# Moving turns, router, adapter and stores at the second and third meeting of sequences

## Chip, core and metric

One NeuronCore of a Trainium2 chip runs the whole kernel in one launch. The metric is the device time of the launch in microseconds (us), lower is better. The kernel is written by hand down to the order in which instructions are issued; each engine works off its own queue in that order, and semaphores let engines wait for each other.

## The reference

The input `x` is four sequences of 1024 rows and 1024 columns in float32. What is computed, cut to the main steps:

```python
x = x + attn(layernorm(x), wq, wk, wv, wo)     # 32 heads of 32, rotary q and k, causal softmax
x = x + ffn(layernorm(x), route_w, A, Bw)

def ffn(x, route_w, A, Bw):                     # 8 experts, rank 16, the best one only
    logits = einsum('bsd,ed->bse', x, route_w)
    topk_v, topk_idx = top_k(logits, 1)
    route_weight = one_hot(topk_idx[..., 0], 8) * topk_v
    h = einsum('bsd,erd->bser', x, A)
    return einsum('bser,eor->bso', route_weight[..., None] * h, Bw)
```

## The kernel before

Each sequence has eight row tiles of 128 rows and eight groups of four heads. A *unit* is one group of one sequence, so there are 32 units. The kernel works on three things at once. In unit u the scores, the exponentials and the products with the values of group u (and the second half of group u - 1) are made. Into them are woven the q, k and v projections of group u + 1. And, from the second sequence on, one row tile per unit of the sequence before is finished: output product with `wo`, residual, second layernorm, turn, router, adapter, store.

The score work of a unit is a fixed list of eleven slots, `SLOTS`: nine score rounds, with the marks "second" and "first" between them, at which half of a group's values are multiplied (`apply`). Everything else is a list of `Step`s, each with a cost in units of about one product; `fill` takes steps from the list `todo` after each slot until that slot's share of the cost is spent. So a step's place in the list decides beside which score round it is issued. A step can also put work on `postponed`: a pair of a cost and a function, and the function is called once steps of that much cost have gone by.

A *meeting* is the last unit of a sequence (group 7), where the next sequence begins. There are three, in units 7, 15 and 23. The second and third have a list written out by hand in `change_steps`, because six kinds of step meet there:

- `norm.find(t)`, `norm.scale(t)`, `norm.turn(t)` for the row tiles of the next sequence: statistics on DVE (with a power on POOL), scaling on DVE (L189), and eight transposes on PE (L201, `pt_a`), copied out of PSUM by ACT (L203, L205). Every turn of a tile loads another one. Tiles 3, 4 and 6 live for a while in the buffers of the coming qT and kT, so the profile shows them as `qT` and `kT`.
- `h`, the held steps: products of the value projection of unit 15 or 23 (`pv`, L337).
- `p`, the project steps: sixteen output products of the last row tile of the old sequence (`po`, L751), eight for each half of the columns. Each uses a weight chunk, loaded from DRAM into one of four buffers; a product asks for the chunk four places on.
- `turn`, `route`, `turn_hidden` and `adapt` of the row tile before that (tile 6). `turn` is `pt_f`; `route` is a product with the router's and the experts' weights (`ph`, L773) and five small steps on DVE that give `wh`; `turn_hidden` transposes `wh` (`pw`, L802); `adapt` makes two products (`pf`, L812), adds them to `y` on DVE (L815) and stores `y` to `out_y` (L816). On SP the store waits for L815.
- the projections of the next unit (`chains`: `pq`, `pk`, `pv`).
- the score rounds and value products (`s`, L430; `av`, L634), which the slots put between them.

All projection, turn, router and adapter results pass through four PSUM banks (pool `ps`), which are given out again as they come free. Scores and value products have a bank area of their own with one buffer.

DVE also finds the maxima of each score round (L462, L483), transposes the probabilities in place (L516) and the values (L1096), and scales the value products (L654). All DMA is issued by one queue, SP, in program order. Values go out to DRAM and come back rearranged (`spread_values`): four stores `vd<-vT` and eight loads `vals<-vd` per unit. In the main loop `stores` holds the stores of a unit's values and value products, and `scatter` puts the eight loads into `todo`, two steps apart.

Of the kernel before, what the change touches and what calls it, by code (L numbers as in the profile page):

```python
# [14 lines left out]
P = 128  # L15
# [56 lines left out]
def tile_preln_attn_then_top1_lora(  # L72
# [17 lines left out]
    nc = tc.nc  # L90
    B, S, D = x.shape
# [5 lines left out]
    NG = HEADS // HG  # L97
# [17 lines left out]
    def bank(shape, name):  # L115
        return ps.tile(shape, F32, tag="ps", name=name)
# [58 lines left out]
    def find_moments(src, name):  # L175
        stats = small.tile([P, D // 512, nc.vector.BN_STATS_DIM], F32, tag="stats", name=f"st_{name}")
        for i in range(D // 512):
            nc.vector.bn_stats(stats[:, i, :], src[:, i * 512 : (i + 1) * 512])
        mv = small.tile([P, nc.vector.BN_AGGR_DIM], F32, tag="mv", name=f"mv_{name}", bufs=3)
        nc.vector.bn_aggr(mv, stats)  # L180
        ve = small.tile([P, 1], F32, tag="ve", name=f"ve_{name}")
        nc.vector.tensor_scalar(ve, mv[:, 1:2], EPS, None, ALU.add)
        rstd = small.tile([P, 1], F32, tag="rstd", name=f"rstd_{name}", bufs=3)
        nc.gpsimd.tensor_tensor(rstd, ve, half_sb, ALU.pow)
        return mv, rstd
# [41 lines left out]
    postponed = []  # L227
# [19 lines left out]
    class Norm:  # L247
# [32 lines left out]
        def find(self, t):  # L280
            while self.found <= t and self.found in self.x:
                k = self.found
                self.moments[k] = find_moments(self.x[k], f"a{self.b}_{k}")
                self.found += 1
# [26 lines left out]
        def scaling(self, t):  # L311
            return Step(lambda: self.scale(t), 0.0)

        def turning(self, t):
            return Step(lambda: self.turn(t), 2.0 if self.b == 0 else 1.3)
# [169 lines left out]
    def release_exps():  # L485
        to_exp.extend(next_exp)
        next_exp.clear()
# [200 lines left out]
    def load_adapter():  # L688

        ra_all = NC * (E + ER)  # L690
        room = big.tile([P, ra_all + D + TB * D], F32, tag="prob0", name="adapter")
        kept["ra"] = room[:, :ra_all].rearrange("p (c n) -> p c n", n=E + ER)
        kept["bw"] = room[:ER, ra_all : ra_all + D]
        for k in range(TB):
            kept[k] = room[:, ra_all + D + k * D : ra_all + D + (k + 1) * D]
        nc.sync.dma_start(kept["ra"], ra.rearrange("(c p) n -> p c n", p=P))
        nc.sync.dma_start(kept["bw"], bw)
# [13 lines left out]
    def take_chunk(n):  # L711
        for k in range(n, n + 4):
            if k < n + 3 or n == 0:
                load_chunk(k)
        return loaded[n]

    def finish_steps(b, t, kind="stream"):
# [88 lines left out]
        def adapt(ks=None):  # L806
            y = st["y"]
            for n in range(2):
                cols = slice(n * 512, (n + 1) * 512)
                pf = bank([P, 512], f"pf_{name}_{n}")  # L810
                rhs = kept["bw"][:, cols] if ks is None else take_chunk(ks[n])
                nc.tensor.matmul(pf, lhsT=st["whT"], rhs=rhs, start=True, stop=True)  # L812
                if ks is not None:
                    load_chunk(ks[n] + 4)
                nc.vector.tensor_tensor(y[:, cols], pf, y[:, cols], ALU.add)  # L815
            nc.sync.dma_start(out[b, t * P : (t + 1) * P, :], y)  # L816

        def number(step, sources):

# [2 lines left out]
        chains = []  # L822
# [27 lines left out]
    def change_steps(u, norm, project, tail, held):  # L850

        p, h, turning, scaling = project, held, norm.turning, norm.scaling
        out, chains = [], []
        for n, tb in (("q", 0), ("k", 0), ("q", 1), ("k", 1), ("v", 0), ("v", 1)):
            chains += chain(u, n, tb)
        if p:
            turn, route, turn_hidden, adapt = tail
            find = norm.finding  # L860
            load_last = Step(lambda: norm.load(7), 0.0)
            out += [*h[:2], turn, *h[2:4], find(3), p[0], h[4], turning(2), h[5], p[1], route, scaling(3)]
            out += [find(4), h[6], p[2], h[7], p[3], turn_hidden, scaling(4), *p[4:6], adapt, load_last]
            out += [p[6], find(5), p[7], turning(3), scaling(5), *p[8:10], turning(4), *p[10:12]]
            chains = weave(chains[:-6], p[12:]) + chains[-6:]
            out += [*chains[:2], find(6), *chains[2:4], scaling(6), turning(5), *chains[4:6], find(7)]
            out += [*chains[6:8], scaling(7), turning(6), *chains[8:14], turning(7)]
            return out + chains[14:]
        for t, n in zip(range(TB, NT), (3, 4, 4, 4)):
            out += [*chains[:n], turning(t)]  # L870
            del chains[:n]
        return out + chains
# [194 lines left out]
    def scatter(steps, apart):  # L1067

        for k, s in enumerate(steps):
            todo.insert(min(len(todo), 1 + apart * k), s)  # L1070

    n_slots = len(SLOTS)
    second, first_ = SLOTS.index("second"), SLOTS.index("first")
    final = len(units) - 1
    for u, (b, g) in enumerate(units):
        do_postponed(math.inf)
        do_postponed(math.inf)
        todo.extend(between[u])
        ends_at = n_slots
        if b + 1 < B and g + 1 == NG:  # L1080
            if b:
                norms[b + 1].load(3, 4)
        if u == final:
            load_wo()
            ends_at = second
        for r, pieces in enumerate(SLOTS):
            if pieces == "second":
                release_exps()
            if pieces == "second":
                if u == final:  # L1090
                    todo.extend(early)
                    ends_at = second + 3
                put, loads = spread_values(u)

                def meanwhile():
                    nc.vector.transpose(vTs[u], vTs[u])  # L1096
                    if u in ahead_of:
                        ahead_of[u][0]()

                if u:  # L1100
                    apply(u - 1, 1, meanwhile)
                else:
                    meanwhile()
                stores.append(put)
            elif pieces == "first":
                apply(u, 0)
                find_tops(u)
                ended.clear()
            else:
                release_exps()  # L1110
                turn_probabilities()
                if second < r < first_:
                    join_sums(u, 0)
                if r == second + 1 and u in ahead_of:
                    ahead_of[u][1]()
                score_round(u, pieces)
                if r == second - 1 and u:
                    while any((u - 1, t) in places for t in range(QT, 2 * QT)):
                        exponentiate_some(1)
                        turn_probabilities()  # L1120
                    join_sums(u - 1, 1)
                if r != first_ - 1:
                    find_tops(u)
                exponentiate_some(SHARE / 3)
                next_exp.extend((u, t, h) for t in ended for h in range(HG))
                if r != first_ - 1:
                    ended.clear()
                if r in (second + 1, first_ + 1):
                    for put in stores:
                        put()  # L1130
                    stores.clear()
                    if u == final and r == first_ + 1:
                        load_adapter()
                if r == second + 2:
                    scatter(loads, 2)
                    if u in late_fetch:
                        do(late_fetch[u])
                        for k in range(3 if b == 1 else 0):
                            load_chunk(k)
            if u == final:  # L1140
                if r == second + 3:
                    todo.extend(parts)
                    ends_at = first_ + 2
                if r == first_ + 1:
                    todo.extend(wholes)
                    ends_at = n_slots + 2
            held_back = APART_BY if r < second else 0
            ahead = LENGTHS if not b and u + 1 < NG else [1.0] * ends_at
            fill(
                ahead[r] / sum(ahead[r:ends_at]),  # L1150
                held_back,
                0.0 if pieces in ("first", "second") else SHARE * 2 / 3,
            )
# [61 lines left out]
```

## Time and profile before

| | |
|---|---|
| median of 3 runs | 2722.84 us (2721.9 to 2724.6) |
| profiled execution | 2722.25 us |
| its span in the trace | 2720.5 us |
| granted TensorE clock, mean | 0.997 |
| PE busy | 2666.9 us, 98% of the span |
| DVE busy | 2143.7 us, 79% |
| ACT busy | 1723.5 us, 63% |
| POOL busy | 601.4 us, 22% |
| weight chunks `chunk<-in_wo` | 368 issues of 256 KB, 3.8 us to landing (median) |
| stores `out_y<-x` | 32 issues of 512 KB, 2.6 us to landing |

The profile's times are of one execution. Engines are PE (TensorE), DVE (VectorE), ACT (ScalarE), POOL (GpSimd) and SP (the queue that issues DMAs). In a timeline row the first number is the start in us from the start of the span, the second the time that the row's instructions took together, then engine, line, operation, what is written and read, shape and count; a bracket gives the idle time of the engine just before and what ended it. A float32 product of 512 columns appears as two MATMUL records. The windows view gives, for each stretch of time, how long each engine was busy in it, and the granted clock of TensorE as a share of full speed.

### The profile page before, as it was taken

Reading aid. Unit: us, or ns where it says so; the run is one execution under the profiler, and the core shown is the slowest. Engines: PE = TensorE matmul, PEld = TensorE weight load, DVE = VectorE, ACT = ScalarE, POOL = GpSimd, SP = SyncE. Lnnn points to the kernel's source line nnn. Section 1 sums busy time; section 2 is a strip of 40 time slices with the busy share of each in tenths; the row PEclk is TensorE's granted clock in tenths of the full one; section 3 lists DMA queues with packets and bytes.
Section 4 is the critical chain, followed back from the end, with each engine's and each line's share of the span. In section 5 each row is a group of like instructions: output and inputs, shape, how many; then the busy total and the mean of one; then the engine's idle time right before and its main releaser. Section 6 shows DMA issues by size and latency. Waiting matters only on the chain.

```text
span 2720.5 us, 84063 instructions
## 1 busy us (share of the span) xinstructions
PE 2666.9 (98%) x35108; PEld 1302.4 (48%) x35108; DVE 2143.7 (79%) x4256; ACT 1723.5 (63%) x4978; POOL 601.4 (22%) x845
## 2 busy tenths in 40 slices
PE   8999999999999999989999999999999999999998
PEld 5444444444444544445444454444544444544445
DVE  4899989887777788887777877888787777787555
ACT  2878777876666676665666666766566666666521
POOL 2222222222222222222122222222212222212000
PEclk9999999999999999999999999999999999999999
DMA  3222223226554445652555454564355555446421
GB/s 119 60 72 73 75 74 81 64 64 172 149 135 134 126 127 155 168 158 65 161 160 134 135 131 133 137 188 135 80 158 149 154 134 138 120 131 199 126 69 53
DMA packets 465900, 332.74 MB, mean 122 GB/s; under 512 B 160880, under 2 KB 382320, under 8 KB 465520
## 3 DMA queue, kind: packets, MB, share of 16 engines
q1 hardware_dynamic: 465520, 327.37, 44.1%
q8 instruction: 276, 4.52, 0.7%
q14 instruction: 104, 0.85, 0.1%
HBM read 277.01 MB, written 50.26 MB: 120 GB/s over the span
## 4 chain that ended last, share of the span: by engine, by line
PE 79%; DVE 13%; DMA 3%; ACT 3%; POOL 1%; issue 1%; SPq 1%; POOLq 0%; DVEq 0%; ACTq 0%
PE po L751 15%; PE pq L337 14%; PE pk L337 13%; PE pv L337 11%; PE s L430 11%; PE av L634 8%; DVE top L462 4%; DVE pr L516 3%; PE ph L773 2%; PE pf L812 2%; DMA chunk<-in_wo 2%; DVE both L483 1%; ACT pr L441 1%; ACT pr L491 1%; PE pt_f L201 1%
## 5 line engine op out<-in xcount | busy, mean ns | idle before, releaser
L491 ACT ACTIVATE pr<-pr,both 128x256 f32<-128x256 f32 (+15 forms) x2048 | 1044.4, 518 | 51.2 <-DVE both L483 51.2
L441 ACT COPY pr<-s 128x640 f32<-128x640 f32 (+14 forms) x544 | 525.1, 1017 | 670.4 <-PE s L430 669.7
L462 DVE TENSOR_REDUCE top<-pr 128x2 f32<-128x960 f32 (+15 forms) x768 | 650.6, 893 | 253.6 <-POOL pr L444 253.0
L516 DVE STREAM_TRANSPOSE pr<-pr 128x1024 f32<-128x1024 f32 (+11 forms) x768 | 664.8, 907 | 34.5 <-ACT pr L491 31.0
L444 POOL TENSOR_TENSOR pr<-pr,causal_sb 128x128 f32<-128x128 f32 x512 | 237.3, 470 | 1166.8 <-ACT pr L441 1158.2
L337 PE MATMUL pv<-xnT,wv 128*128 128x512 f32 x1024 | 486.3, 602 | 0.0
L337 PE MATMUL pq<-xnT,wq 128*128 128x512 f32 x1008 | 478.2, 602 | 0.2 <-ACT xnT L203 0.2
L337 PE MATMUL pk<-xnT,wk 128*128 128x512 f32 x1008 | 477.9, 603 | 0.0
L430 PE MATMUL s<-kT,qT 32*32 32x256 f32 (+4 forms) x17408 | 394.5, 385 | 8.9 <-POOL pr L444 3.0
L491 ACT ACTIVATION_READ_ACCUMULATOR pr<-pr,both 128x1 f32 x2048 | 401.3, 196 | 0.0
L751 PE MATMUL po<-chunk,attn 128*128 128x512 f32 x736 | 379.2, 600 | 7.5 <-DMA chunk<-in_wo 7.5
L430 PEld LDWEIGHTS s<-kT,qT 32*32 32x32 f32 x17408 | 187.6, 103 | 267.4 <-issue 102.7
L337 PEld LDWEIGHTS pk<-xnT,wk 128*128 128x128 f32 x1008 | 181.4, 190 | 234.9 <-issue 234.5
L337 PEld LDWEIGHTS pq<-xnT,wq 128*128 128x128 f32 x1008 | 183.3, 191 | 225.1 <-issue 223.8
L337 PEld LDWEIGHTS pv<-xnT,wv 128*128 128x128 f32 x1024 | 185.6, 190 | 218.1 <-issue 216.6
L634 PE MATMUL av<-pr,vals 64*32 64x256 f32 (+3 forms) x12288 | 272.0, 319 | 4.6 <-DVE pr L516 3.8
L634 PEld LDWEIGHTS av<-pr,vals 64*32 64x32 f32 x12288 | 214.1, 106 | 112.3 <-issue 66.4
L483 DVE TENSOR_TENSOR both<-top 32x4 f32<-32x4 f32 (+3 forms) x1152 | 207.8, 180 | 23.8
L751 PEld LDWEIGHTS po<-chunk,attn 128*128 128x128 f32 x736 | 134.8, 190 | 173.7 <-issue 147.7
L654 DVE TENSOR_TENSOR at<-av,by 128x256 f32<-128x256 f32 x128 | 48.2, 418 | 108.7 <-PE av L634 70.4
L751 PE MATMUL po<-wo,attn 128*128 128x512 f32 x256 | 116.6, 596 | 0.0
L375 POOL TENSOR_TENSOR qT<-qT,swapq 128x512 f32<-128x512 f32 x64 | 81.6, 1274 | 140.0 <-DVE swapq L371 140.0
(89 smaller groups left out, 1561.9 us busy)
## 6 DMA issues: line engine op xcount, KB each, us to landing
chunk<-in_wo SPq DMA_DIRECT2D x368, 256.0 KB, 3.8
vals<-vd SPq DMA_DIRECT2D x256, 128.0 KB, 4.3
x<-in_x SPq DMA_DIRECT2D x56, 512.0 KB, 6.2
wq<-in_wq SPq DMA_DIRECT2D x32, 512.0 KB, 4.4
wk<-in_wk SPq DMA_DIRECT2D x32, 512.0 KB, 4.2
wv<-in_wv SPq DMA_DIRECT2D x32, 512.0 KB, 4.4
vd<-vT SPq DMA_DIRECT2D x128, 128.0 KB, 4.6
out_y<-x SPq DMA_DIRECT2D x32, 512.0 KB, 2.6
```

Source lines behind the costliest of these rows:

```text
L337: nc.tensor.matmul(at["p"], lhsT=wt[:, c, :], rhs=xnTs[b, tb][:, c, :], start=(c == 0), stop=(c == NC - 1),)
L375: nc.gpsimd.tensor_tensor(dst[:, cols], dst[:, cols], other, ALU.add)
L430: nc.tensor.matmul(sc[i * SQ : (i + 1) * SQ, h, at : at + w].rearrange("p (j k) -> p j k", k=SQ), lhsT=of_q[rows, 2 * t + half], rhs=of_k[ ...
L441: nc.scalar.copy(pr[:, :, k0 : k0 + w], sc[:, :, at : at + w])
L444: nc.gpsimd.tensor_tensor(diagonal, diagonal, causal_sb.unsqueeze(1).to_broadcast([P, HG, SQ]), ALU.add)
L462: nc.vector.tensor_reduce(top[:, k, h : h + step], places[u, t][:, h : h + step, :], AX.X, ALU.max, negate=True,)
L483: nc.vector.tensor_tensor(dst[rows], src[rows], src[other], op)
L491: nc.scalar.activation(pr[:, h, :], pr[:, h, :], AF.Exp, bias=tops[u, t][:, h : h + 1], accum_out=dens[u, t // QT][:, t % QT, h : h + 1],)
L516: nc.vector.transpose(pr, pr)
L634: nc.tensor.matmul(avs[half][h * HD : (h + 1) * HD, t0:, :], lhsT=v[rows, j, h * HD : (h + 1) * HD], rhs=rhs, start=(j == 0), stop=(j == n ...
L751: nc.tensor.matmul(st["po"], lhsT=lhsT, rhs=rhs, start=(c == start), stop=(c == stop))
L773: nc.tensor.matmul(ph, lhsT=st["ynT"][:, c, :], rhs=w[:, c - i * RA, :], start=(c == 0), stop=(c == NC - 1),)
```

## The change

It has four parts.

1. In `change_steps` the hand-written list of the second and third meeting is put in another order. The steps are the same. The turn of tile 2 stands behind two more steps; `route` stands behind project steps 1, 2 and 3 instead of step 1; `adapt` stands behind project step 6 instead of 5; the load of tile 7 comes three project steps later; in the next unit's projections the score round that lies there meets tile 5's turn already done, tile 6 is scaled one step of `chains` before the place where it was and tile 7 is scaled behind the turn of tile 6 instead of ahead of it.
2. `adapt` no longer stores `y` at once where the weights are streamed (`ks` is given): the store goes on `postponed` with a cost of 4.5. This holds for all finished tiles of the first three sequences, not only at the meetings.
3. In the last unit of the second and third sequence (`meet`) the stores on `stores` are issued one score round later.
4. In the same units the eight value loads are scattered into `todo` one round later.

In the built program the order of instructions differs at the two meetings, and on SP for the stores of the tiles finished in the units next to them and in the last two units. Elsewhere each engine's order is as before, and no instruction is added or removed.

```diff
@@ adapt
-            nc.sync.dma_start(out[b, t * P : (t + 1) * P, :], y)
+            def store():
+                nc.sync.dma_start(out[b, t * P : (t + 1) * P, :], y)
+            if ks is None:
+                store()
+            else:
+                postponed.append([4.5, store])
@@ change_steps
-            out += [*h[:2], turn, *h[2:4], find(3), p[0], h[4], turning(2), h[5], p[1], route, scaling(3)]
-            out += [find(4), h[6], p[2], h[7], p[3], turn_hidden, scaling(4), *p[4:6], adapt, load_last]
-            out += [p[6], find(5), p[7], turning(3), scaling(5), *p[8:10], turning(4), *p[10:12]]
+            out += [*h[:2], turn, *h[2:4], find(3), p[0], h[4], p[1], h[5], turning(2), h[6], p[2], h[7]]
+            out += [p[3], route, scaling(3), find(4), p[4], p[5], turn_hidden, scaling(4), p[6], adapt]
+            out += [find(5), p[7], p[8], turning(3), scaling(5), p[9], load_last, p[10], turning(4), p[11]]
             chains = weave(chains[:-6], p[12:]) + chains[-6:]
-            out += [*chains[:2], find(6), *chains[2:4], scaling(6), turning(5), *chains[4:6], find(7)]
-            out += [*chains[6:8], scaling(7), turning(6), *chains[8:14], turning(7)]
+            out += [*chains[:2], find(6), chains[2], scaling(6), chains[3], turning(5), *chains[4:6]]
+            out += [find(7), *chains[6:8], turning(6), scaling(7), *chains[8:14], turning(7)]
@@ main loop
-                if r in (second + 1, first_ + 1):
+                meet = b and b + 1 < B and g + 1 == NG
+                if r in (second + (2 if meet else 1), first_ + 1):
                     for put in stores:
                         put()
...
+                if r == second + (3 if meet else 2):
+                    scatter(loads, 2)
                 if r == second + 2:
-                    scatter(loads, 2)
                     if u in late_fetch:
```

## The prediction

> **What bounds the kernel now.** I read the page first, then PE's waits by place, then the order of time of PE, DVE and the SP queue around them, then the granted clock. On the page TensorE (PE) is busy nearly all the time, so only its gaps can be won:
>
> ```profile
> PE 2666.9 (98%) x35108; PEld 1302.4 (48%) x35108; DVE 2143.7 (79%) x4256; ACT 1723.5 (63%) x4978; POOL 601.4 (22%) x845
> ```
>
> A span of 2720.5 less 2666.9 leaves 53.6 us. The change reorders PE only where sequences 1 and 2 meet (near 1160 us) and 2 and 3 (near 1835 us). PE's timeline of the first meeting, the rows with a wait (in brackets: us idle before the row, and what ended it):
>
> ```profile
> 1164.98 1.14 PE L201 MATMUL pt_a<-eye_sb,x 128*128 128x128 f32 x8 [1.39 <-ACT yn L203]
> 1179.52 0.33 PE L802 MATMUL pw<-eye_sb,wh 128*128 128x128 f32 x1 [0.51 <-DVE wh L792]
> 1188.99 0.66 PE L201 MATMUL pt_a<-eye_sb,qT 128*128 128x128 f32 x4 [0.68 <-ACT xnT L203]
> 1195.46 1.12 PE L751 MATMUL po<-chunk,attn 128*128 128x512 f32 x2 [1.23 <-DMA chunk<-in_wo]
> 1197.50 1.13 PE L751 MATMUL po<-chunk,attn 128*128 128x512 f32 x2 [0.92 <-DMA chunk<-in_wo]
> 1209.85 1.07 PE L201 MATMUL pt_a<-eye_sb,qT 128*128 128x128 f32 x8 [2.26 <-DVE qT L189]
> ```
>
> Sum 6.99. The second meeting has 2.12, 0.52, 0.68, 1.43 and 2.26 at the same places (7.01). So at most about 14 us stand to be won. But DVE, in the same stretch, has no gap over 0.7 us from 1145 to 1192.7; these are its rows before the adapter's sums (L815):
>
> ```profile
> 1179.18 0.29 DVE L792 TENSOR_TENSOR wh<-ph,gate 128x128 f32<-128x128 f32 x1
> 1179.38 0.80 DVE L189 TENSOR_SCALAR qT<-qT,mv_a,rstd_a 128x1024 f32<-128x1024 f32 x1
> ...
> 1181.73 1.24 DVE L516 STREAM_TRANSPOSE pr<-pr 128x1024 f32<-128x1024 f32 x1
> 1182.89 1.20 DVE L1096 STREAM_TRANSPOSE vT<-vT 128x1024 f32<-128x1024 f32 x1
> 1184.02 0.78 DVE L189 TENSOR_SCALAR kT<-kT,mv_a,rstd_a 128x1024 f32<-128x1024 f32 x1
> 1185.14 0.76 DVE L654 TENSOR_TENSOR at<-av,by 128x256 f32<-128x256 f32 x2 [0.35 <-ACT by L606]
> 1185.81 2.70 DVE L516 STREAM_TRANSPOSE pr<-pr 128x896 f32<-128x896 f32 x3
> 1188.44 1.25 DVE L815 TENSOR_TENSOR x<-pf,x 128x512 f32<-128x512 f32 x2
> ```
>
> So up to 1190 PE's waits are DVE's debt: products moved forward only reach DVE's results earlier. After 1193 DVE has slack, and waits there can really go.
>
> **The change, walked on the first meeting** (start to start, in us, from where PE is first idle, 1163.59). The built order has the same instructions; what moves is priced by its own rows.
>
> *Turn of tile 2 and router, later.* PE now does an output product 0.86, scores 1.58, value product 0.96, turn 1.07, then 0.94, 0.86, 0.96, 0.86 and the router 1.85: 1173.53. The turn's PSUM bank, freed by the copy of yn at 1164.93, is free by 1167.0: the wait of 1.39 is gone. The next step, probabilities times values, needs DVE's fourth transpose, which starts at 1173.51 and takes 0.74: a new wait of about 0.5. The step is through at 1177.75. Two products (0.96, 0.86) reach pw at 1179.57, after wh (1179.47): the 0.51 is gone. With pw 0.17, a product 0.90, the second piece 2.29, the reciprocals' turn 0.50, the adapter 1.72 and two products 1.75, PE stands at the turn of tile 3 at 1186.90 (1187.71 before).
>
> *Adapter, later, and the banks.* The banks rotate otherwise: in the built program the two halves of tile 3's turn now wait for the two sums of L815, which empty pf. DVE's chain to them: from 1179.38 transposes 1.16 and 1.13, scaling of tile 3 0.73, statistics 1.55, then 0.81 for the power on POOL (ve_f at 1153.83, scaling at 1154.64), which the two transposes hid before, scaling of tile 4 0.75, then L654 0.67, three transposes 2.63, first sum 0.62: 1189.43. ACT doesn't delay this: the exponentials that the last of the three transposes needs end at 1186.9 by their rows, it starts at 1188.0; POOL idled 5.9 before the power. So PE waits about 2.6 at tile 3, the largest new cost; the old 0.68 there (second half on its own first half's copy) goes. Then halves 0.50 and 0.55, products 1.8, scores 1.84, turn of tile 4 1.05, a product 0.9: PE begins q of the next sequence at 1196.2, against 1198.46: 2.3 gained.
>
> *Stores.* Before, out_y stands on SP at 1189.71 behind L815, with two weight chunks queued behind it; they go out at 1190.64 and PE waits 1.23 and 0.92 for them. Now these chunks stand ahead and go when their buffers are released by pf and the product behind it, by 1186.0; they land in 3.2 to 3.8 (the medians) and are needed from 1190.6 on: both waits gone. If they took the longest landing, 6.9, the last would come at 1192.9, still ahead of 1195.3. Behind the store now stand chunk 160, tile 7 and later loads, none needed for 10 us. The other moved SP entries: wk goes out some 3 us earlier, right behind the last value product; the router's last piece is issued at 1169.95 and takes 2.7 to 2.9 (in_ra's medians), needed at 1173.0: 0 to 1 of wait, hidden by the 0.5 that PE then owes DVE. In the other units the order on SP is the same; in the last two the store falls behind loads that nobody waits for: zero.
>
> *Tile 6 scaled ahead of a round, tile 5 turned ahead of scores.* Before, scaling of tile 6 stood on DVE behind the maxima of the next scores, which costs 2.26. Now: scores end at 1194.25, their maxima 5.0 later as before (1193.14 to 1198.14), so 1199.25; statistics, power and scaling 3.1: 1202.4. The tile's load goes at 1190.6 and took 6.8 (1191.95 to 1198.77): 1197.4, 1.8 ahead of its statistics. PE comes at 1196.2 + 3.53 + 1.07 + 1.07 + 3.53 = 1205.4: no wait. Tile 7, scaled later now, is ready at 1211.0 and needed at 1212.8. After the turn PE stands at 1206.4 against 1210.76: **4.4 gained**. Behind that no PE wait follows until 1317, so it stays.
>
> *Values written and loaded a round later.* Seven of the eight loads now stand behind a router chunk that is released at 1211; at 0.47 each and 3.3 to land they are in by 1218, and needed at 1229.7: zero, 11 us of cover.
>
> *Second meeting.* The DVE rows lie 672.24 later (1185.14, 1857.38), and DVE sets PE's place at tile 3, so PE comes out at 1878.6. Before it was at 1882.0 without the slow clock: **3.4 gained**.
>
> *The clock.* The windows view of the second meeting (PE, PEld, DVE, ACT, POOL busy, then the granted clock, DMA):
>
> ```profile
> 1877.70:1881.10 3.40, 1.15 (x3) 0.21 (x2) 3.22 (x8) 2.94 (x13) 0.00 (x0) 1.00 0.62 172
> 1881.20:1884.60 3.40, 3.40 (x10) 1.93 (x10) 2.60 (x5) 1.78 (x6) 1.78 (x2) 0.50 0.88 150
> ```
>
> Behind a stretch with 2.26 idle follow 3.4 us at half clock: 1.7 lost. The same clock rows show it behind stretches with 2.60, 2.34 and 1.61 idle, not behind 1.64 or 1.45, and not at the first meeting's 2.26, which fell astride two stretches (1.11, 1.15). So this 1.7 goes, and the new waits of 2.6 can each cost 1.7. A 2.6 wait leaves at least 1.62 in one stretch in 8 cases of 10, at least 2.26 in 4 of 10; I take 0.7, nearer the row that tripped at 1.61: 2 x 0.7 x 1.7 = 2.4. The Trainium skill, "TensorE: Matmul & The Clock Gate", section "What's actually happening", says the clock falls after at least one idle window of some 3.4 us; by it no wait here would trip, and the sum would be 2712.7. The trace disagrees: 2.26 idle sufficed.
>
> Sum: -4.4 - 3.4 - 1.7 + 2.4 = -7.1. The profiled execution took 2722.25 (span 2720.5; the median of the runs is 0.6 above): **2715.2**.
>
> **Rivals.**
> *More of it eaten (no change to tell).* DVE's chain to L815 is long; if it runs 1 us later than summed, or tile 6 again meets a wait of 1 to 2, each meeting gives 1 to 2 less, and both clock drops come: -7.8 - 1.7 + 3.4 + 3 = -3.1, 2719.2. For: seven DVE steps in a row, each on another engine's result. Against: they are the same rows, and the cover behind them is 3 us.
> *No new slow stretch:* neither new wait trips the clock (0.3 x 0.3 = 0.09 by the rows): -9.5, 2712.7. If also the wait at tile 3 were not there, 5.2 more at most: 2707.5. Against: the built program's waits name L815. This first case is also what the rule of the Trainium skill above would give.
> *Slower: the value loads.* SP issues in order, and seven loads stand behind a chunk that PE releases in mid-round. It decides once that release comes after 1222 instead of 1211 (last load out 3.3 later, landed 3.3 after that: past 1229). From there each us costs one at each meeting; 6.5 late at both gives 2715.2 + 13 = 2728.2. Against: the 11 us.
> *The change does nothing:* excluded by the order, which moves.
>
> **How the numbers follow.** Forecast with one or two slow stretches 0.53; less slow clock or a smaller wait 0.09; eaten 0.30; slower 0.08 (the value loads, or another queue the walk missed). 0.2% of 2722.84 is 5.4 us, about what a measurement of this kernel can tell from no change: faster means under 2717.4. Forecast and better cases are faster: 0.62; same 0.30; slower 0.08. The range runs from a case between 2712.7 and 2707.5 to the worse end of the eaten one: 2711 to 2721.
>
> **What would show it.** Right: at each meeting PE waits of about 0.5 (1.2 at the second, where PE comes 0.7 earlier) on DVE's L516 and about 2.6 on L815 ahead of tile 3, none on chunks, none on tile 6; L337's q chain 2.3 earlier, k 4.4. Wrong: a chunk wait at po, a wait at av for vals, tile 3 without a wait, or a wait over 3.5 there.

## The result, and the profile after

| | before | after |
|---|---|---|
| median | 2722.84 us (2721.24 to 2725.87, 5 runs) | 2710.74 us (2709.1 to 2716.06, 5 runs) |
| ratio, 95% interval | | 0.996 (0.9949 to 0.9971) |
| profiled execution, its span | 2722.25, 2720.5 | 2710.74, 2709.0 |
| PE busy | 2666.9 | 2664.0 |

The kernel became faster, by 12.1 us here and by 10.3 in a repeat further down (2709.77 against 2720.07, ratio 0.9959, 0.9945 to 0.9972). The forecast was 2715.2, about 7 us; the median lies 0.3 below the low end of the range. The page's line of busy times of after:

```profile
PE 2664.0 (98%) x35108; PEld 1300.3 (48%) x35108; DVE 2143.4 (79%) x4256; ACT 1723.6 (64%) x4978; POOL 601.9 (22%) x845
```

Counts are the same, so nothing was saved in work; 11.5 us of span went, 2.9 of it out of PE's busy time (one half-clock stretch less is 1.7 of that), the rest out of its gaps. PE's timeline of after, the rows with a wait, first meeting:

```profile
1169.70 2.31 PE L773 MATMUL ph<-chunk,yn 128*128 128x136 f32 x16 [0.67 <-ACT xnT L203]
1187.80 1.25 PE L201 MATMUL pt_a<-eye_sb,qT 128*128 128x128 f32 x8 [2.30 <-DVE x L815]
1204.56 1.98 PE L337 MATMUL pk<-xnT,wk 128*128 128x512 f32 x4 [0.18 <-ACT rawq L363]
```

and the second:

```profile
1839.53 4.32 PE L634 MATMUL av<-pr,vals 64*32 64x256 f32 x128 [0.18 <-DVE pr L516]
1855.35 1.30 PE L201 MATMUL pt_a<-eye_sb,qT 128*128 128x128 f32 x8 [2.31 <-DVE x L815]
1873.81 1.98 PE L337 MATMUL pk<-xnT,wk 128*128 128x512 f32 x4 [0.18 <-ACT rawq L363]
```

Six waits of 6.99 and five of 7.01 have become three each, of 3.15 and 2.67 in all. No row waits for a chunk (`po<-chunk`, 1.23, 0.92 and 1.43 before), none for the scaling of tile 6 (2.26 before), and one large new wait stands in front of tile 3 (`qT`), on the adapter's sums. DVE's rows up to those sums, first meeting:

```profile
1177.53 0.29 DVE L792 TENSOR_TENSOR wh<-ph,gate 128x128 f32<-128x128 f32 x1
1177.74 1.24 DVE L516 STREAM_TRANSPOSE pr<-pr 128x1024 f32<-128x1024 f32 x1
1178.90 1.20 DVE L1105 STREAM_TRANSPOSE vT<-vT 128x1024 f32<-128x1024 f32 x1
1180.02 0.77 DVE L189 TENSOR_SCALAR qT<-qT,mv_a,rstd_a 128x1024 f32<-128x1024 f32 x1
...
1183.09 0.81 DVE L189 TENSOR_SCALAR kT<-kT,mv_a,rstd_a 128x1024 f32<-128x1024 f32 x1 [0.67 <-POOL rstd_a L184]
1183.81 0.75 DVE L654 TENSOR_TENSOR at<-av,by 128x256 f32<-128x256 f32 x2
1184.48 2.69 DVE L516 STREAM_TRANSPOSE pr<-pr 128x896 f32<-128x896 f32 x3
1187.09 1.25 DVE L815 TENSOR_TENSOR x<-pf,x 128x512 f32<-128x512 f32 x2
```

It is a chain without a gap but the one for the power on POOL (0.67), as the prediction wrote it out. PE stood ready at 1185.50 and started at 1187.80, when the first of the two sums had emptied its bank.

Where the 11.5 us of span went, by marks on PE. A meeting is measured from the turn of tile 6 of the old sequence (`pt_f`, 1159.13 before, 1156.76 after) to the next `pt_f`:

| stretch | before | after | difference |
|---|---|---|---|
| start to first meeting | 1159.1 | 1156.8 | -2.4 |
| first meeting | 108.3 | 104.5 | -3.7 |
| between | 563.2 | 563.7 | +0.5 |
| second meeting | 109.7 | 105.5 | -4.1 |
| behind it | 780.1 | 778.4 | -1.7 |

The meetings gave 7.9. The other 3.6 lie where the order on PE is the same in both kernels; the first two experiments show that differences of that size come and go there without the change.

### The profile page after: what moved, and what is told of

Read it like the earlier page. It is cut to its first block, busy times and chain, and to the rows that moved or that the text cites. A ratio compares the mean times of both kernels' runs of the same rounds, so it can differ in the third digit from the quotient of the medians.

```text
span 2709.0 us, 84062 instructions
## 1 busy us (share of the span) xinstructions
PE 2664.0 (98%) x35108; PEld 1300.3 (48%) x35108; DVE 2143.4 (79%) x4256; ACT 1723.6 (64%) x4978; POOL 601.9 (22%) x845
## 4 chain that ended last, share of the span: by engine, by line
PE 80%; DVE 13%; ACT 3%; DMA 1%; issue 1%; POOL 1%; SPq 1%; POOLq 0%; DVEq 0%; ACTq 0%
PE po L751 15%; PE pq L337 14%; PE pk L337 14%; PE pv L337 12%; PE s L430 11%; PE av L634 8%; DVE top L462 4%; DVE pr L516 4%; PE ph L773 2%; PE pf L812 2%; ACT pr L491 1%; DVE both L483 1%; ACT pr L441 1%; PE pt_f L201 1%; DVE st_a L178 1%
## 5 line engine op out<-in xcount | busy, mean ns | idle before, releaser
L462 DVE TENSOR_REDUCE top<-pr 128x2 f32<-128x960 f32 (+15 forms) x768 | 650.7, 894 | 251.4 <-POOL pr L444 250.8
L516 DVE STREAM_TRANSPOSE pr<-pr 128x1024 f32<-128x1024 f32 (+11 forms) x768 | 664.7, 908 | 34.1 <-ACT pr L491 30.7
L483 DVE TENSOR_TENSOR both<-top 32x4 f32<-32x4 f32 (+3 forms) x1152 | 207.4, 180 | 23.8
L654 DVE TENSOR_TENSOR at<-av,by 128x256 f32<-128x256 f32 x128 | 48.2, 418 | 107.2 <-PE av L634 60.4
```

What stands on the lines that cost most here:

```text
L462: nc.vector.tensor_reduce(top[:, k, h : h + step], places[u, t][:, h : h + step, :], AX.X, ALU.max, negate=True,)
L483: nc.vector.tensor_tensor(dst[rows], src[rows], src[other], op)
L516: nc.vector.transpose(pr, pr)
```

## The experiments

Each was timed in five rounds or more beside the kernel before on the same chip. "Meetings" are the two stretches of the table above in the profiled execution; "half clock" counts the half-clock stretches in them. PE's waits are those of the two meetings.

| kernel | median us | before, same chip | ratio (95%) | meetings | PE's waits | half clock |
|---|---|---|---|---|---|---|
| before | 2722.84 | | | 218.0 | 6.99 + 7.01 | 1 |
| before_again | 2721.29 | 2721.14 | 1.0004 (0.9995 to 1.0014) | 220.5 | 7.26 + 7.26 | 3 |
| rounds_only | 2721.23 | 2721.14 | 1.0002 (0.9993 to 1.0011) | 219.5 | 7.22 + 7.66 | 2 |
| late6 | 2721.43 | 2721.31 | 0.9999 (0.999 to 1.0008) | 218.8 | 6.25 + 5.96 | 3 |
| tile6_only | 2716.57 | 2721.68 | 0.9983 (0.9973 to 0.9993) | 214.0 | 6.18 + 5.37 | 0 |
| store_only | 2716.16 | 2721.14 | 0.9981 (0.9972 to 0.9989) | 212.9 | 5.07 + 4.78 | 1 |
| later_before | 2715.54 | 2721.31 | 0.9981 (0.9972 to 0.999) | 216.1 | 5.79 + 5.45 | 2 |
| store_tile6 | 2711.14 | 2721.68 | 0.996 (0.9947 to 0.9972) | 210.1 | 3.58 + 3.88 | 1 |
| after | 2710.74 | 2722.84 | 0.996 (0.9949 to 0.9971) | 210.1 | 3.15 + 2.67 | 1 |
| reorder_only | 2710.45 | 2721.14 | 0.9964 (0.9952 to 0.9975) | 210.3 | 3.33 + 2.95 | 1 |
| after_again | 2709.77 | 2720.07 | 0.9959 (0.9945 to 0.9972) | 211.4 | 2.83 + 3.36 | 2 |
| scale_back | 2709.27 | 2721.68 | 0.9956 (0.9943 to 0.9968) | 210.5 | 2.99 + 3.15 | 1 |
| later_old_front | 2707.03 | 2721.31 | 0.995 (0.9936 to 0.9963) | 207.4 | 2.75 + 2.25 | 1 |
| later_turns | 2705.2 | 2721.68 | 0.994 (0.9928 to 0.9953) | 203.9 | 0.74 + 0.84 | 0 |

**before_again and after_again: the same two kernels once more.** No edit.

> The kernel before, unchanged, measured against itself. If the gain that the walk did not hold (the trace of after is 2.4 us ahead of before's when it enters the first meeting, and 1.7 us more at the end) is chance, this kernel's own trace differs from the first one's by as much: 1 to 3 us in the time at which it enters the meeting, and another set of stretches at half clock; its time is that of before within 2 us. If that gain belongs to the change, this trace enters the meeting within 0.5 us of 1159.1 (pt_f of the first meeting).

> The changed kernel unchanged, once more, to part what the change does from what one profiled execution happens to hold. Theory: the two meetings take 104 to 106 us each (104.5 and 105.6 in the first profile), with the same waits (2.30 on L815 at both, none at tile 6 nor on chunks), while the place of the first meeting (1156.8) and the half-clock stretches outside the meetings differ by a few us; the median is 10 to 11 below the kernel before. By the prediction's own sum the median would be 7 below. Rival: the 3.6 us that the first profile showed outside the meetings belong to the change; then the first meeting begins near 1156.8 and the end behind the second takes 778.4 again.

The first meeting began at 1154.3 in the repeat of before and at 1159.1 in the first profile of it; over all fourteen profiled executions, whose PE has the same order up to there, it began between 1153.8 and 1164.2. So -2.4 at that place is what one execution happens to hold, and not the change. The stretch behind the second meeting took 778.5 in the repeat of after and 778.4 the first time, which is what the rival named; but reorder_only, which leaves the stores alone, has 778.3 there and later_before, which has only one small edit at the meetings, 778.6, while later_turns, which holds the whole change, has 780.3. So that is not the change either; in before_again, rounds_only and later_turns, which have 780.3 to 781.3 there, the clock fell some 699 us behind the second meeting, in the others it didn't (before has 780.1 without it). The two meetings of after_again took 105.2 and 106.3, the second 0.3 more than expected. The repeat also says that the first profile of before was a light one in the meetings: one half-clock stretch there, three in the repeat. The mean of the three executions with the order of before is 219.3 (before, before_again, rounds_only), of the two of after 210.8: the meetings give 8.5.

**reorder_only: the hand-written list alone (part 1).**

```diff
@@ change_steps: the new order of the list, as in the change
   (adapt stores at once; stores and loads of values in their old rounds)
```

> Only the new order of steps at the second and third meeting; stores at once and value stores and loads at their old rounds. Theory (waits of the meetings): the order alone takes away the waits on the yn copies, on wh and on tile 6; the chunks that wait behind the store are 158 and 159, which go out at about 1188.7 and are needed at 1193.5 and later, so the chunk waits go too; the new wait of 2.3 on L815 stays. Gain as of the whole change less at most 1: 9 to 12 us under before. Rival (the stores past loads make the gain, in all units): 4 to 6 us under before, with chunk waits at the meetings.

It has the whole gain, and no wait for a chunk, though the store still stands where it stood behind the sums:

```profile
1168.40 2.12 PE L773 MATMUL ph<-chunk,yn 128*128 128x136 f32 x16 [0.68 <-ACT xnT L203]
1170.69 4.32 PE L634 MATMUL av<-pr,vals 64*32 64x256 f32 x128 [0.17 <-DVE pr L516]
1186.49 1.25 PE L201 MATMUL pt_a<-eye_sb,qT 128*128 128x128 f32 x8 [2.30 <-DVE x L815]
1203.26 1.98 PE L337 MATMUL pk<-xnT,wk 128*128 128x512 f32 x4 [0.18 <-ACT rawq L363]
```

These are after's waits at that meeting and one of 0.17 more. Its SP queue shows why (SPq is the time in which the queue issued):

```profile
1176.95 5.88 SPq L708 DMA_DIRECT2D chunk<-in_wo  x4
1187.06 0.34 SPq L816 DMA_DIRECT2D out_y<-x  x1
1187.50 1.22 SPq L708 DMA_DIRECT2D chunk<-in_wo  x2
```

The two chunks still go out behind the store, at 1187.5, but the wait of 2.30 at tile 3 now stands ahead of the products that use them. The store and the wait at tile 3 hang on the same two sums, so PE is held back together with the chunks: it comes to the first product that uses them at 1192.17, 4.7 after that chunk went out, where before it came 3.6 after (1190.64, 1194.23) and waited 1.23.

**store_only: the later store alone (part 2).**

```diff
@@ adapt
-            nc.sync.dma_start(out[b, t * P : (t + 1) * P, :], y)
+            def store():
+                nc.sync.dma_start(out[b, t * P : (t + 1) * P, :], y)
+            if ks is None:
+                store()
+            else:
+                postponed.append([4.5, store])
```

> Only the store of finished tiles postponed by five products. Theory: it takes away the chunk waits at the two meetings (2.15 and 1.43) and nothing else, and PE comes that much earlier to the rest: 2.5 to 4 us under before, with the waits on the yn copies (1.4, 2.1), wh (0.5) and tile 6 (2.3) still there. Rival (stores make the gain in all units): 7 us or more under before.

5.0 us by the medians, more than the 2.5 to 4 that were expected; in waits it is 4.2 less than the first profile of before had (9.85 against 14.0). The rows with a wait at its first meeting:

```profile
1166.26 1.14 PE L201 MATMUL pt_a<-eye_sb,x 128*128 128x128 f32 x8 [1.62 <-ACT yn L203]
1180.80 0.33 PE L802 MATMUL pw<-eye_sb,wh 128*128 128x128 f32 x1 [0.51 <-DVE wh L792]
1190.26 0.66 PE L201 MATMUL pt_a<-eye_sb,qT 128*128 128x128 f32 x4 [0.68 <-ACT xnT L203]
1208.45 1.83 PE L201 MATMUL pt_a<-eye_sb,qT 128*128 128x128 f32 x8 [2.26 <-DVE qT L189]
```

Exactly the chunk waits are gone, at both meetings. So the prediction's step on the stores is right of the store by itself; beside the new list it is spare, since the list removes the same waits.

**rounds_only: values written and loaded a round later (parts 3 and 4).**

```diff
@@ main loop
+                meet = b and b + 1 < B and g + 1 == NG
-                if r in (second + 1, first_ + 1):
+                if r in (second + (2 if meet else 1), first_ + 1):
...
+                if r == second + (3 if meet else 2):
+                    scatter(loads, 2)
                 if r == second + 2:
-                    scatter(loads, 2)
```

> Only the value stores and loads of units 15 and 23 one score round later. Theory: no wait of PE stands on them, so the time is that of before within 1 us. Rival: the value transfers run beside the chunk loads that PE waits for, so the chunk waits (1.23, 0.92; 1.43) shrink and the time falls by 2 to 3.5 us.

Nothing: 1.0002. In after the last seven value loads are issued from 1209.94 to 1213.38 and take 3.7 to land (median of the eight); the products that need them start at 1228.00. The cover is 10.9 us, where the prediction had 11.

**scale_back: the two `chains` lines of before in the changed kernel.**

```diff
@@ change_steps
-            out += [*chains[:2], find(6), chains[2], scaling(6), chains[3], turning(5), *chains[4:6]]
-            out += [find(7), *chains[6:8], turning(6), scaling(7), *chains[8:14], turning(7)]
+            out += [*chains[:2], find(6), *chains[2:4], scaling(6), turning(5), *chains[4:6], find(7)]
+            out += [*chains[6:8], scaling(7), turning(6), *chains[8:14], turning(7)]
```

> The changed kernel with the last two lines of the order as before: tile 5 turned behind the scores, tile 6 scaled behind their maxima, tile 7 scaled ahead of tile 6's turn. Theory: the wait of 2.26 on tile 6's scaling is back at both meetings, the rest stays: 4.5 us over the changed kernel, or 6 where the clock falls behind it (2715 to 2717, 4 to 6 under before). Rival (PE's earlier arrival alone removed it): within 1 us of the changed kernel.

This expectation missed: 2709.27, no slower than after. Its DVE rows say why:

```profile
1199.07 0.81 DVE L189 TENSOR_SCALAR qT<-qT,mv_a,rstd_a 128x1024 f32<-128x1024 f32 x1 [0.73 <-PE s L430]
1199.79 0.70 DVE L516 STREAM_TRANSPOSE pr<-pr 128x512 f32<-128x512 f32 x1
1201.53 2.35 DVE L462 TENSOR_REDUCE top<-pr 128x2 f32<-128x1024 f32 x2 [1.03 <-POOL pr L444]
```

Tile 6 (`qT`) is scaled ahead of the maxima (L462) here too. A slot takes steps by cost, and the lines in front have shifted the list so far that the old text of these two lines puts the scaling ahead of the round all the same. On PE and SP this kernel has after's order; on DVE only the scaling of tile 7 changes places with one step of q. The edit had not undone what it was meant to undo.

**late6: tile 6 really behind the maxima again.** The same two lines, one more place on, so that on DVE the scaling alone falls behind the maxima; the order on PE and SP is after's.

```diff
@@ change_steps
-            out += [*chains[:2], find(6), chains[2], scaling(6), chains[3], turning(5), *chains[4:6]]
+            out += [*chains[:2], find(6), *chains[2:4], turning(5), scaling(6), *chains[4:6]]
```

> The changed kernel, with one thing undone on VectorE alone: at both meetings the scaling of tile 6 stands again behind the maxima of the next score round, with its statistics left where they were and PE's order untouched. In the changed kernel these maxima end at 1205.5 and PE comes to tile 6 at 1203.3; scaling takes 0.73. If the prediction's step is right (a wait in front of tile 6 is due to this place on VectorE alone), PE waits about 3.0 (1206.3 less 1203.3) on L189 at tile 6 at each meeting, and tile 7 stays early enough: 2 x 3.0, and up to 1.7 of half clock behind each: 2716 to 2720 against 2710.7. Rival: the place doesn't matter, because the product chains behind it, or tile 7, or the copies of rawq would make PE wait as long in any case: 2710 to 2713.

On DVE the scaling now stands behind seven others: one transpose (L516), two searches for maxima (L462) and the four steps that combine them (L483). The wait came as priced, 3.09 at both meetings:

```profile
1189.62 1.71 PE L201 MATMUL pt_a<-eye_sb,qT 128*128 128x128 f32 x8 [2.30 <-DVE x L815]
1210.04 1.41 PE L201 MATMUL pt_a<-eye_sb,qT 128*128 128x128 f32 x8 [3.09 <-DVE qT L189]
```

The time is 1.4 above the range of that expectation; in the profiled execution the meetings took 8.7 more than after's (two waits of 3.09 and two more half-clock stretches make 9.6). And the ratio to before is 0.9999: **one instruction of DVE at each meeting, put back behind seven others, takes all of the change's gain.** PE's waits at the first meeting sum to nearly what they were before (6.25 against 6.99): the other moves alone only gather six waits into two large ones and two small. They can even cost: store_only also scales tile 6 late, but has the old places of turn, router and adapter, and is 5.3 faster than late6 by the medians (2716.16, 2721.43; on two chips). Its waits are 2.4 less (9.85 against 12.21), and its profile has two half-clock stretches less in the meetings.

**tile6_only and store_tile6: the kernel before with the two new `chains` lines, and with these and the later store.** Both keep the old places of turn, router and adapter.

```diff
@@ change_steps
-            out += [*chains[:2], find(6), *chains[2:4], scaling(6), turning(5), *chains[4:6], find(7)]
-            out += [*chains[6:8], scaling(7), turning(6), *chains[8:14], turning(7)]
+            out += [*chains[:2], find(6), chains[2], scaling(6), chains[3], turning(5), *chains[4:6]]
+            out += [find(7), *chains[6:8], turning(6), scaling(7), *chains[8:14], turning(7)]
@@ adapt (store_tile6 alone)
+                postponed.append([4.5, store])
```

> The kernel before with only those two lines new. Theory: the wait of 2.26 on tile 6 goes at both meetings, the waits on yn copies, wh, tile 3's bank and chunks stay: 4.5 us under before, up to 6 with the clock. Rival (PE then waits on tile 7 or on the maxima instead): 0 to 2 us under before.

> The kernel before with those two lines and the postponed store, but turn of tile 2, router, adapter, tiles 3 and 4 in their old places. Theory (DVE's debt: moving turn, router and adapter trades waits of 1.39, 0.51 and 0.68 for 0.67 and 2.30): within 1 us of the whole change, 9 to 11 us under before, without any wait on L815. Rival (moving turn, router and adapter is worth what it removes, 2.6 and 3.3): 4 to 6 us slower than the whole change.

Tile 6 alone gives 5.1, the later store alone gave 5.0, both together give 10.5, the whole of the change. At the second meeting of store_tile6 the old waits in front are all there:

```profile
1831.34 1.14 PE L201 MATMUL pt_a<-eye_sb,x 128*128 128x128 f32 x8 [2.04 <-ACT yn L203]
1845.89 0.33 PE L802 MATMUL pw<-eye_sb,wh 128*128 128x128 f32 x1 [0.52 <-DVE wh L792]
1855.36 0.66 PE L201 MATMUL pt_a<-eye_sb,qT 128*128 128x128 f32 x4 [0.68 <-ACT xnT L203]
1872.80 1.12 PE L337 MATMUL pk<-xnT,wk 128*128 128x512 f32 x2 [0.64 <-ACT rawq L363]
```

3.88 in all against 2.67 in after, and the same time. So, beside the two other parts, moving turn, router and adapter trades these for the 2.30 at L815 and gains next to nothing: what PE wins there it pays back to DVE at the sums.

**later_turns: the debt paid on DVE.** If DVE's chain to the sums is what PE waits for, it must be shortened, not PE's order changed. The last three transposes ahead of the sums (L516, 2.69) are not needed for them; here they go behind.

```diff
-    def apply(u, blk, meanwhile=lambda: None):
+    def apply(u, blk, meanwhile=lambda: None, later=False):
...
-        turn_probabilities()
+        if not later:
+            turn_probabilities()
...
-                    apply(u - 1, 1, meanwhile)
+                    apply(u - 1, 1, meanwhile, b and b + 1 < B and g + 1 == NG)
```

> The changed kernel, and at the second and third meeting the three transposes of probabilities (L516, 2.63 us) that DVE does between L654 and the adapter's sums (L815) come behind those sums instead. Theory (DVE's queue sets the wait at tile 3): L815 comes 2.6 us earlier, so the wait of 2.30 at tile 3 falls to under 0.6 (chunks 156 and 157, whose buffers pf frees, may show up to 0.8 in its place), and the transposes fit into DVE's gap of 2.26 before the next maxima; 1.5 to 2.3 us less at each meeting, and the clock no longer falls there: 3 to 6 us under the changed kernel (some 2705 to 2708 where before is 2721). Rival (the wait is the bank's or the chunks' whatever DVE does): under 1 us less.

2705.2, the best of all, 0.994 (0.9928 to 0.9953) of before; on its own chip 16.5 below it. DVE and PE of its first meeting:

```profile
1184.56 0.75 DVE L654 TENSOR_TENSOR at<-av,by 128x256 f32<-128x256 f32 x2
1185.23 1.28 DVE L815 TENSOR_TENSOR x<-pf,x 128x512 f32<-128x512 f32 x2
```

```profile
1170.42 2.39 PE L773 MATMUL ph<-chunk,yn 128*128 128x136 f32 x16 [0.56 <-ACT xnT L203]
...
1186.08 1.14 PE L201 MATMUL pt_a<-eye_sb,qT 128*128 128x128 f32 x8
```

The sums stand right behind L654, and tile 3 starts without a wait. 0.74 and 0.84 of waiting are left at the two meetings, and no half-clock stretch.

**later_before and later_old_front: the same edit in the kernel before, and in store_tile6.** The diff is the one of later_turns.

> The kernel before, with only the three last transposes of probabilities (L516, 2.63 in all) put behind the adapter's sums on VectorE at both meetings. If VectorE's debt is what paces this stretch, the sums, the store and the two weight chunks behind it come 2.6 earlier: the chunk waits (2.15 and 1.43) go, the waits of 1.39 to 2.12 in front, and 2.26 at tile 6, stay: 3 to 4 less, 2717 to 2719. Rival: the maxima come 1.1 later in return (VectorE was idle 1.5 ahead of them, the transposes take 2.6) and eat it at tile 6: 2720 to 2722.

> The kernel before with the store later and tile 6 scaled ahead (measured 2711.1), and the three transposes put behind the adapter's sums, so all of the best version but the new places of turn, router and adapter. If the sums' place matters only where the new order makes PE wait for them, nothing is won here: no wait in this kernel names L815; 2710 to 2712, the 2.1 and 0.7 in front stay, and the new places are then worth the difference to the best version's 2705.2. Rival: the transposes' place is worth 5 by itself, whatever the order: 2705 to 2707.

By the medians both gave more than the first theory of each had it: 5.8 below before instead of 3 to 4, and 2707.03 instead of 2710 to 2712. By the meetings it is less: 3.2 in later_before (216.1 against the mean of 219.3), which is what its theory had, and 2.8 in later_old_front (207.4 against 210.1); the rest of both is not assigned. In later_before one chunk wait is left at each meeting (1.05 and 1.15), so the sums' place didn't remove all of 2.15 and 1.43; but the half-turn wait of 0.68 at tile 3 went as well, at both meetings and in both kernels. In before its row names ACT's copy of the first half, and rightly: the second half starts at 1188.99, right behind the end of that copy (1188.94) and ahead of the end of the first sum (1189.09). Why the wait goes once the sums come earlier is open; most likely the second half is then given another PSUM bank, which no view here shows. It is 1.4 of the 2.8 in later_old_front, and 0.95 is a shorter wait at the turn of tile 2 in the second meeting (1.09 against 2.04). With the transposes out of the way the new places of turn, router and adapter are worth 1.8 by the medians (2707.03 to 2705.2, on two chips) and 3.5 by the meetings (207.4 to 203.9), of which 1.7 is a half-clock stretch that later_turns doesn't have. The intervals of the two ratios overlap (0.9936 to 0.9963, 0.9928 to 0.9953), so this gain is likely and not shown.

## Why the prediction was right, and where it was off

**"Up to 1190 PE's waits are DVE's debt":** right of the place at which PE comes out behind the sums. Moving PE's steps gained 1.2 of waiting at the second meeting and no time (store_tile6 against after); taking 2.69 of transposes out of DVE's chain gained 5.5 and took the wait away (later_turns); the same edit gained 5.8 in the old order by the medians and 3.2 by the meetings (later_before). It is not right of each wait by itself: the one at the turn of tile 2 stayed in later_before (1.96 and 1.53), and its row names ACT's copy.

**Turn of tile 2 and router:** 1.39 is gone, as stated, and 0.51 too. The new wait was forecast on DVE's transposes, 0.5 and 1.2 at `av`; at the first meeting it came one step earlier, 0.67 at `ph`, on the copy of tile 2 by ACT. The walk had followed the banks to the turn and to tile 3, but not to the router. At the second it was 0.18 at `av`. The sums by the walk (1.7) and measured (0.67 and 0.18) differ by 0.8 to 0.9. By the walk's own figures (a transpose from 1173.51 that takes 0.74, PE there at 1173.53) its 0.5 would have been 0.7.

**Adapter, banks, tile 3:** right; 2.30 and 2.31 where 2.6 was forecast, on the line that was named. The old 0.68 there went.

**Stores:** the chunk waits are gone, as stated. That the store was needed for it is not so: in the built order the wait on L815 covers the chunks anyhow (reorder_only).

**Tile 6:** right. Alone it is worth as much as the later store (5.1 and 5.0), and without it the rest of the change together is worth nothing (late6). No wait stands there in after. The turn of tile 6 starts at 1203.34 against 1209.85; less the 2.37 by which this execution was ahead already (1159.13 less 1156.76), that is 4.1 gained where 4.4 was forecast, and q starts 1.8 earlier (1194.34 against 1198.46, less 2.37) where 2.3 was. What the prediction didn't see is that the front lines alone already move this scaling (scale_back).

**The two meetings** without the clock: forecast 4.4 and 3.4. Measured 3.7 and 4.1, each meeting's own half-clock stretches being none and none in the first, one and one in the second. The sum is 7.9 against 7.8. With 1.7 taken off for each half-clock stretch, the three executions with the order of before and the two of after give 4.0 and 3.7.

**Values a round later:** zero, as stated.

**The clock:** the term that failed. It stood as -1.7 for the one stretch that the profile of before showed and +2.4 for two new ones, +0.7 in all. Both parts were mis-sized. Over three profiled executions the order of before has 1, 3 and 2 half-clock stretches in its meetings, mean 2.0; that of after 1 and 2, mean 1.5. At 1.7 each that is -0.9, and the sum -8.7; the meetings measured -8.5 (219.3 to 210.8). The windows view of after's second meeting shows such a stretch behind the new wait (PE, PEld, DVE, ACT, POOL busy, then the granted clock, DMA share and GB/s):

```profile
1849.70:1853.10 3.40, 3.33 (x8) 1.14 (x6) 2.70 (x7) 2.65 (x11) 0.55 (x1) 1.00 0.41 130
1853.10:1856.50 3.40, 1.16 (x9) 0.98 (x10) 3.40 (x7) 0.46 (x1) 0.00 (x0) 0.99 0.54 181
1856.50:1859.90 3.40, 3.40 (x5) 0.95 (x4) 2.37 (x5) 0.71 (x2) 0.55 (x1) 0.51 0.54 120
```

PE idled 2.24 of the middle stretch, and the next one ran at 0.51. The same wait at the first meeting fell across two stretches (1.91 in the longer) and no half clock followed. In the repeat of after both tripped. The rule of the Trainium skill, "TensorE: Matmul & The Clock Gate", section "What's actually happening", that the clock falls after at least one idle window of some 3.4 us, is against these rows, as it was against those of before.

**The level:** the sum was set against one profiled execution. By the medians the gain is 10.3 to 12.1, in the meetings 8.5; the 1.8 to 3.6 between them is not assigned. The medians of the kernel before alone differ by 2.8 (2720.07 to 2722.84 in five comparisons). The low end of the range missed the median by 0.3 for want of this and of the clock. With the clock term as measured, the forecast would have been 2713.6 (2722.25 less 8.7).

**The rivals:** *more of it eaten* did not come: DVE's chain ended 0.7 later than summed (tile 3 starts at 1187.80, plus 2.37 is 1190.17, against 1189.43), not 1, and tile 6 was scaled 2.5 us before PE came to it (1200.84, 1203.34). late6 shows what its other half costs. *No new slow stretch* (2712.7) came in half: one of the two waits tripped the clock in the first profile of after, both in the repeat. *The value loads* are excluded by rounds_only.

## What to carry to other kernels

Waits that stand in a row on one engine can be one debt of another engine, as here: moving the waiting engine's work forward then only collects them in fewer places (six waits of 6.99 became two large and two small ones of 6.25, late6), and the place to work on is the other engine's queue, by what stands ahead of the released result without being needed for it (three transposes, 5.5 us). Where a list is filled into slots by cost, an edit's text doesn't tell what it moves; look at the built order of every engine, of an undo too. And a gain that hangs on threshold events such as the granted clock should be summed from several profiled executions, not from one.

## What the runs showed of the hardware that was not expected

The prediction put the half clock behind stretches with 1.61 of idle time or more, and set the chance of a wait of 2.6 at 0.7. The fourteen profiled executions are sharper. Between 10 and 2690 us from the start of the span, cut into the stretches of 3.413 us on which the granted clock changes, counted from the half-clock rows of each execution (in before they stand 113, 511 and 745 such stretches behind the first), PE's idle time in a stretch (records of matmuls alone) and what followed stand like this:

| idle in the stretch | stretches | followed by half clock |
|---|---|---|
| 2.0 us or more | 46 | 46 |
| 1.6 to 2.0 | 30 | 5 |
| 1.2 to 1.6 | 46 | 0 |
| 0.3 to 1.2 | 338 | 0 |

So what counts is how much of a wait falls into one stretch of 3.413: here 2.0 or more always tripped, and under 1.6 never. A wait of 2.3 puts 2.0 or more into one stretch in about half of the places it can fall (it lies wholly inside for 1.11 of 3.413, and with 0.3 or less cut off at either end for 0.6 more), which is what the five executions with the wait of 2.30 at tile 3 (after, after_again, reorder_only, scale_back, late6) show: six of their ten waits were followed by half clock. Why five of the stretches between 1.6 and 2.0 tripped and 25 did not is open. A wait of over 2 us can thus cost up to 1.7 more than its length (half of 3.413), which pieces of under 1.6, each in a stretch of its own, did not.
